# Cross attention's division: sums and weighted values copied off their banks by ScalarE, reciprocals in pairs over two steps

## Chip, core and metric

The kernel runs on one core of a Trainium2 chip. The metric is the device time of one execution in microseconds (us); before the change it is 1362.8 us, the median of three runs (1362.6 to 1363.32).

The core has engines that run side by side, each with its own list of instructions that it takes strictly in order: TensorE (PE; its weight loads are shown as PEld), VectorE (DVE), ScalarE (ACT), GpSimd (POOL), and SyncE (SP), which here issues DMA transfers. An instruction waits until what it needs is there, and everything behind it in its list waits with it. PE writes its results into banks of PSUM; a bank can be used again when the engine that reads it has read it.

## The reference, cut to what matters

A decoder layer in float32 on x of 16 batches x 112 tokens x 512: self attention, cross attention to a context of 375 tokens a batch, and a gated feed-forward network (FFN) with a Walsh-Hadamard transform. The change lies in the cross attention:

```python
q = proj(hs, Wq, bq, S)          # hs: layer norm of x; 16 heads of 32
k = proj(at, Wk, bk, T)          # at: the context, T = 375
v = proj(at, Wv, bv, T)
scores = einsum('bhsd,bhtd->bhst', q, k) / sqrt(32)
scores = clip(scores, -50.0, 50.0)
scores = where(attend, scores, -10000.0)
scores = clip(scores, -50.0, 50.0)
probs = softmax(scores, axis=-1)
probs = probs / (probs.sum(axis=-1, keepdims=True) + 1e-08)
ctx = einsum('bhst,bhtd->bhsd', probs, v)
delta = rs * (ctx @ Wo.T + bo)   # then a layer norm of delta, added to x
```

The kernel does not divide each probability. It multiplies the exponentials by the values, sums the exponentials over the 375 tokens, and multiplies the weighted values by the reciprocal of the sums and by 1/(1 + 1e-8).

## The kernel before

The program has three stretches: self attention (to about 300 us in the profile), cross attention (300 to 843 us), FFN (to the end). The order of PE's instructions is written by hand (a manual schedule, for PE alone): it is the order in which the program's lines are run. The order on the other engines comes from a scheduler, which goes by what is ready and by the order in the program; `tc.issue_after(x)` tells it not to place something ahead of instruction x.

In the cross attention the main loop goes over 16 batches b, and in a batch over three steps kc, each with 125 of the 375 context tokens (KC = 3, KP = 125). A head's 32 features lie in a group of 32 partitions, so that weighted values and sums are tiles of 128 partitions x 4 x 112 (C = 4, S = 112). One call of `Cross.step(b, kc)` does the following.

- PE makes the scores (L925) into two tiles of PSUM ("sc").
- ACT makes two exponentials from them (L1326, into es at kc = 0, into e otherwise) and two checks (L1330), which count scores beyond the limit in place; when both are done, the score banks are free.
- PE adds the weighted values of the step before ("late") to the bank "ys" (`weigh`, L936). There is one such bank.
- DVE adds the exponentials of the step before to those of its batch's first step (`add`, L1356, two instructions).
- When the step before was a batch's last, `divide` follows, so it stands in the step kc = 0 of the next batch: PE makes the sums over tokens (`key_sums`, L947) into one of three "mm" banks; DVE takes four reciprocals of it (L1368) into r, and multiplies the "ys" bank, the constant and r into xyT (L1369), the input of the output projection; ACT checks r (L1377).
- `f.fill(us)` then lets PE do some microseconds of other work, in pieces that all go through the three "mm" banks: the next batch's values (L898, copied from their bank to v by DVE at L903), its keys in seven products (L1005; DVE takes their results at L1058, L1069, L1082, L1086, L1089 and L1092), queries (L880, copied by ACT at L888), output projections of finished batches (L909), transposes of normalised rows (L841, L842), and products for half a W2 matrix of the FFN (L1627, copied by DVE at L1628).

DVE does more in the meantime: the sums of context quarters that the seven products want (L975), the norms' statistics and steps (L772, L773, L780 to L798, L1283 to L1295), and, in every step after `cross.last` (the last L1356), pieces of work on W2. For batches below 9 these are butterflies on half a W2 (L1643, L1644); at the end of each half SP stores it (L1649, and for the first half L1651), and DVE's L975 for a later batch, which uses a tile of the same pool, waits for that store. SP also loads the next half (L1616) and the context of a later batch (cT, L1214). From batch 9 on they are pieces of W2 (`W2Piece`): SP loads four quarters into w2i (L1660), DVE makes six combinations (L1671, L1674, L1677, L1680, L1683, L1686), SP stores each (L1669). L1671 is the first of a piece and so the one that waits for the loads; the loads wait until the piece before has done with the tile.

After the last step of batch 15, `weigh`, `add` and `divide` are called once more, and the FFN begins.

Of the kernel before, what the change touches and what calls it, by code (L numbers as in the profile page):

```python
# [14 lines left out]
AF = mybir.ActivationFunctionType  # L15
ALU = mybir.AluOpType
# [3 lines left out]
B, S, D = 16, 112, 512  # L20
# [3 lines left out]
C = D // P  # L24
# [6 lines left out]
GB = 4  # L31
# [572 lines left out]
def finite_layer(  # L604
# [30 lines left out]
    nc = tc.nc  # L635
# [12 lines left out]
    def psum(tag, shape, bufs=None):  # L648
        bufs = bufs or banks_of.get(tag, 2)
        return ps[""].tile(shape, F32, tag=tag, bufs=bufs, name=tag)  # L650
# [7 lines left out]
    def pair(name, tag="e", bufs=3):  # L658
        return evp.tile([P, 2, HG, S], F32, tag=tag, name=name, bufs=bufs)
# [66 lines left out]
    xyT = keep.tile([P, C, NT], F32, name="xyT")  # L726
# [9 lines left out]
    low, top = zero[:, : 2 * B * KC], zero[:, 2 * B * KC :]  # L736
    limit = keep.tile([P, 2], F32, name="limit")
# [70 lines left out]
    class Norm:  # L808


        def __init__(self, l, tiles):
            self.l, self.tiles = l, tiles
# [104 lines left out]
    def scores(k_of, q_of, rows_):  # L917

        scs = [psum("sc", [P, 2, 512]) for _ in range(2)]
        views = [  # L920
            s[:rows_, :, : HG * S].rearrange("p i (j s) -> p i j s", j=HG) for s in scs
        ]
        for j in range(C):
            for i in range(HG):
                nc.tensor.matmul(  # L925
                    views[i // 2][:, i % 2, j, :], k_of(i, j), q_of(i, j), start=True, stop=True
                )
        return views
# [16 lines left out]
    def key_sums(sums, es, n):  # L945
        for i in range(HG):
            nc.tensor.matmul(  # L947
                sums[ts(i, DH), :, :], ones[:n, :DH], es[i // 2][:n, i % 2], start=True, stop=True
            )
# [194 lines left out]
    class SelfAttention:  # L1144
# [35 lines left out]
        def step(self, b, grp, f, us, whole):  # L1180
            b, v, es = self.next
            if b + 1 < B:
                self.begin(b + 1, grp)
            first = max(0.45 * us, min(us, 5.5))
            f.fill(first)
            eTs = []
            for e, share in zip(es, (0.45 * (us - first), 0.35 * (us - first))):
                tr = psum("sc", [P, 2, 512])
                trv = tr[:S, :, : HG * S].rearrange("p i (j s) -> p i j s", j=HG)
                for i in range(2):  # L1190
                    for j in range(C):
                        nc.tensor.transpose(trv[:, i, j, :], e[:, i, j, :], ident[:S, :S])  # L1192
                eT = pair("eT")
                nc.scalar.copy(eT[:S], trv)
                eTs.append(eT)
                f.fill(share)
            y = psum("ys", [P, C, S])
            weighted_values(y, v[b % GB][:S], eTs, True, True)
            nc.scalar.copy(xyT[:, :, ts(b, S)], y)
            if whole:  # L1200
                f.drain()
            else:
                f.fill(0.2 * (us - first))
# [103 lines left out]
    class Cross:  # L1307
# [1 line left out]


        def __init__(self):
            self.late = None

        def step(self, b, kc, q, keys, f, us):
            scs = scores(
                lambda i, j: keys.k[ds(i * DH, DH), j, ts(kc, KP)],
                lambda i, j: q[ds(i * DH, DH), j, ts(b % 2, S)],
                KP,
            )
            n = b * KC + kc  # L1320
            late = self.late

            es = [(pair("es", "es", 3) if kc == 0 else pair("e"))[:KP] for _ in scs]
            self.late = (b, kc, keys.v[kc][:KP], es)
            for i, sc in enumerate(scs):
                nc.scalar.activation(  # L1326
                    es[i], sc, AF.Exp, scale=scl[:, n : n + 1], bias=bia[:, n : n + 1]
                )
            for i, sc in enumerate(scs):
                nc.scalar.activation(  # L1330
                    sc,
                    sc,
                    AF.Relu,
                    scale=nscl[:, n : n + 1],
                    bias=limit[:KP, :1],
                    accum_out=low[:KP, 2 * n + i : 2 * n + i + 1],
                )
            self.weigh(late)
            for i in range(2):
                self.add(late, i)  # L1340
            self.divide(late)
            f.fill(us)

        def weigh(self, late):
            if late is None:
                return
            b, kc, v, es = late
            if kc == 0:
                self.y = psum("ys", [P, C, S])
                self.es = es  # L1350
            weighted_values(self.y, v, es, kc == 0, kc == KC - 1)
# [8 lines left out]
        def divide(self, late):  # L1360
            if late is not None and late[1] == KC - 1:
                sums = psum("mm", [P, C, S])
                key_sums(sums, self.es, KP)

                b = late[0]
                r = ln.tile([P, C, S], F32, tag="r", name="r")
                for c in range(C):
                    nc.vector.reciprocal(r[:, c], sums[:, c])  # L1368
                nc.vector.scalar_tensor_tensor(  # L1369
                    xyT[:, :, ts(b, S)],  # L1370
                    in0=self.y,
                    scalar=1.0 / (1.0 + 1e-8),
                    in1=r,
                    op0=ALU.mult,
                    op1=ALU.mult,
                )
                nc.scalar.activation(  # L1377
                    r, r, AF.Relu, scale=-1.0, bias=limit[:, 1:], accum_out=top[:, b : b + 1]
                )

# [353 lines left out]
    for g in range(2, NG):  # L1736
        b = (g - 1) * GB
# [26 lines left out]
    cross = Cross()  # L1764
# [17 lines left out]
    for b in range(B):  # L1782
# [7 lines left out]
        if bl == 0:  # L1790
# [3 lines left out]
            elif g < 3:  # L1794
                c = AfterCross(whole[g - 1], n3[g - 1])
# [40 lines left out]
    cross.add(cross.late, 0)  # L1836
    cross.add(cross.late, 1)
    cross.divide(cross.late)
    ev.close()
    banks.close()  # L1840
    banks_of.update({"mm": 2, "ys": 2})
# [27 lines left out]
    def at_once(pieces):  # L1869
        run(pieces)  # L1870
        yield from ()

    def tiles_of(pieces):

        for _ in pieces:
            next(pieces, None)
            yield

    def tiles_of(pieces):
# [5 lines left out]
    late = itertools.chain(  # L1885
        itertools.repeat(None, 1),
        n3[2].transposes(),
        tiles_of(after[1].projections()),
        at_once(after[1].finish()),
        itertools.repeat(None, 3),  # L1890
        n3[3].transposes(),
    )
# [40 lines left out]
@with_exitstack  # L1933
def decoder_layer(ctx: ExitStack, tc: tile.TileContext, *args):
    nc = tc.nc
    flag = ctx.enter_context(tc.tile_pool(name="flag", bufs=1))
    unfit = flag.tile([1, 1], I32, name="unfit")
    finite_layer(tc, unfit, *args)
    with tc.If(nc.values_load(unfit, min_val=0, max_val=1, skip_runtime_bounds_check_because="a comparison gives 0 or 1") > 0):
        general_layer(tc, *args)  # L1940
# [49 lines left out]
```

## Time and profile before

| what | value |
|---|---|
| median of three runs | 1362.8 us |
| the profiled execution | 1362.72 us, its span 1360.9 us |
| granted PE clock, mean | 0.998 |
| cross attention, 300 to 843 us | 543.0 us, of them PE 539.1 busy, DVE 365.5, ACT 239.2 |
| reciprocals L1368 | 64, 795 ns median |
| product L1369 | 16, 624 ns median |
| check of r, L1377 | 16, 668 ns and 186 ns for its accumulator |
| exponentials L1326, checks L1330 | 1094 ns and 1068 ns mean |
| copy of values L903 | 0.68 us |

How to read it: the span is what the profiler shows between the first and the last instruction; the time of the execution is a little longer. A row of a timeline gives the start in us, the duration, engine and line, operation, the tile written and those read, the shape, how many in a row, and in brackets how long the engine was idle before it and what ended that. The name of a releaser is inferred from semaphores. PE's busy time is made of matmuls whose ends are modelled, so that a stall of under about a tenth of a microsecond can hide in it.

### The profile page before, as it was taken

The page shows a single profiled execution, that of the slowest core. Times are in us where ns is not written, and L with a number is a line of the kernel's source. Part 1 is how long each engine was busy: PE and PEld are TensorE (multiplying, and loading weights), DVE is VectorE, ACT ScalarE, POOL GpSimd, SP SyncE. Part 2 cuts the span into 40 slices and gives each one's busy share as a digit, 9 for nine tenths or more (in the row PEclk, how much of TensorE's full clock was granted, in tenths as well). Part 3 has the DMA queues.
Part 4 walks back from the last instruction along what each step waited for, and adds up shares of the span by engine and source line. Part 5 has one row for each costly group of instructions (what it writes and reads, how often), then busy time and mean ns, then how long its engine had stood idle before and what let it go on. Part 6 is the DMA issues. An engine that isn't in the chain of part 4 may idle for free.

```text
span 1360.9 us, 20404 instructions
## 1 busy us (share of the span) xinstructions
PE 1340.7 (99%) x8472; PEld 834.1 (61%) x8472; DVE 820.6 (60%) x1571; ACT 440.6 (32%) x859; POOL 38.0 (3%) x68
## 2 busy tenths in 40 slices
PE   8999999999999999999999999999999999999997
PEld 5587776665767577756777765545555555555553
DVE  4487768735565686669675668557653245554332
ACT  3355453643444334433545452201110011111000
POOL 2000100310000100000000000000000000000000
PEclk9999999999999999999999999999999999999999
DMA  7000022110103011103342111111031122322201
GB/s 249 1 1 1 22 80 71 31 47 24 55 24 124 16 55 62 55 1 109 108 136 97 39 48 32 47 46 47 32 124 62 47 62 70 92 77 79 92 0 57
DMA packets 63898, 82.44 MB, mean 61 GB/s; under 512 B 3105, under 2 KB 48177, under 8 KB 61365
## 3 DMA queue, kind: packets, MB, share of 16 engines
q1 hardware_dynamic: 62128, 77.83, 17.4%
q0 software_dynamic: 672, 1.62, 0.4%
q8 instruction: 69, 1.13, 0.3%
q10 hardware_dynamic: 996, 1.59, 0.3%
q14 instruction: 33, 0.26, 0.1%
HBM read 65.83 MB, written 15.20 MB: 60 GB/s over the span
## 4 chain that ended last, share of the span: by engine, by line
PE 94%; DVE 4%; ACT 1%; DMA 1%; issue 1%; DVEq 0%; ACTq 0%; POOLq 0%
PE mm L898 15%; PE mm L1005 14%; PE gate L1538 12%; PE mm L909 7%; PE ys L1538 7%; PE gate L1472 6%; PE mm L880 6%; PE mm L1538 5%; PE sc L925 5%; PE ys L936 4%; PE ys L1472 4%; PE mm L1472 3%; PE sc L1192 2%; PE mm L841 1%; PE mm L1627 1%; PE mm L947 1%
## 5 line engine op out<-in xcount | busy, mean ns | idle before, releaser
L898 PE MATMUL mm<-xv,cT 128*125 128x512 f32 x384 | 178.8, 602 | 0.8 <-DVE v L903 0.8
L1326 ACT ACTIVATE e<-sc,bia,scl 125x896 f32<-125x896 f32 x64 | 68.4, 1094 | 171.3 <-PE sc L925 171.3
L898 PEld LDWEIGHTS mm<-xv,cT 128*125 128x125 f32 x384 | 68.4, 187 | 76.4 <-issue 71.8
L1330 ACT ACTIVATE sc<-sc,limit,nscl 125x896 f32<-125x896 f32 x96 | 102.6, 1068 | 0.0
L1538 PE MATMUL gate<-t,f 128*128 128x448 f32 x256 | 101.5, 539 | 0.0
L1356 DVE TENSOR_TENSOR es<-es,e 125x896 f32<-125x896 f32 x64 | 68.4, 1090 | 49.1 <-ACT e L1326 49.1
L1472 PE MATMUL gate<-h,f 128*128 128x448 f32 x224 | 86.6, 540 | 0.0
L1538 PE MATMUL gate<-xyT,f 128*128 128x448 f32 x192 | 80.1, 540 | 0.0
L1538 PEld LDWEIGHTS gate<-t,f 128*128 128x128 f32 x256 | 48.8, 190 | 47.4 <-issue 46.9
L1162 ACT ACTIVATE e<-sc,mx 112x112 f32<-112x112 f32 x256 | 64.3, 402 | 41.7 <-DVE mx L1158 41.7
L1538 PE MATMUL ys<-t,f 128*128 128x448 f32 x192 | 77.4, 539 | 0.0
L1005 PEld LDWEIGHTS mm<-kt,xks 128*128 128x128 f32 x360 | 59.1, 190 | 15.3 <-issue 14.8
L1472 PEld LDWEIGHTS gate<-h,f 128*128 128x128 f32 x224 | 42.6, 190 | 41.2 <-issue 40.8
L1554 ACT COPY u<-gate 128x448 f32<-128x448 f32 x16 | 8.5, 531 | 182.3 <-PE gate L1538 109.4
L1005 PE MATMUL mm<-kt,xks 128*128 128x188 f32 x360 | 63.5, 324 | 0.0
L1538 PEld LDWEIGHTS ys<-t,f 128*128 128x128 f32 x192 | 36.6, 190 | 35.6 <-issue 35.4
L1484 DVE TENSOR_TENSOR h<-h,h 128x896 f32<-128x896 f32 x32 | 32.8, 1086 | 40.9 <-PE ys L1472 31.6
L1538 PEld LDWEIGHTS gate<-xyT,f 128*128 128x128 f32 x192 | 36.1, 190 | 34.3 <-issue 33.7
L898 PE MATMUL mm<-wv,xyT 128*112 128x512 f32 x128 | 56.9, 595 | 0.0
L925 PEld LDWEIGHTS sc<-q,kT 32*125 32x125 f32 x1536 | 46.2, 183 | 15.5 <-issue 13.2
L925 PE MATMUL sc<-q,kT 32*125 32x112 f32 x1536 | 54.7, 279 | 0.0
L1538 PE MATMUL mm<-xyT,f 128*128 128x448 f32 x128 | 53.4, 540 | 0.0
(237 smaller groups left out, 2211.2 us busy)
## 6 DMA issues: line engine op xcount, KB each, us to landing
f<-in_f_w SPq DMA_DIRECT2D x64, 256.0 KB, 3.2
f<-blocks SPq DMA_DIRECT2D x14, 1024.0 KB, 4.8
cT<-in_ctx SPq DMA_DIRECT2D x16, 750.0 KB, 4.8
w<-in_f_w SPq DMA_DIRECT2D x4, 1024.0 KB, 6.1
w<-w SPq DMA_DIRECT2D x4, 1024.0 KB, 4.6
w2i<-w SPq DMA_DIRECT2D x16, 256.0 KB, 4.1
blocks<-w2o SPq DMA_DIRECT2D x12, 256.0 KB, 2.4
blocks<-w2i SPq DMA_DIRECT2D x12, 256.0 KB, 2.4
```

What stands on the lines that cost most here:

```text
L880: nc.tensor.matmul(acc[:, :n], w[:, c, ts(j, P)], src[:, c, :], start=(c == 0), stop=(c == C - 1))
L898: nc.tensor.matmul(acc[:n, :], src[:, c, :], w[:, c, :], start=(c == 0), stop=(c == C - 1))
L909: nc.tensor.matmul(acc, xyT[:, c, ts(t, P)], w[:, c, :], start=(c == 0), stop=(c == C - 1))
L925: nc.tensor.matmul(views[i // 2][:, i % 2, j, :], k_of(i, j), q_of(i, j), start=True, stop=True)
L936: nc.tensor.matmul(y[ts(i, DH), j, :], v[:, HG * j + i, :], es[i // 2][:n, i % 2, j, :], start=first and j == 0, stop=last, skip_group_che ...
L1005: nc.tensor.matmul(acc[:, m], lhs[:, k, ts(m, P)], rhs[:, k], start=first and m == 0 and k == 0, stop=k == 1, skip_group_check=True,)
L1162: nc.scalar.activation(e[:, i, j, :], sc[:, i, j, :], AF.Exp, scale=SCALE, bias=mx[:, i, j : j + 1],)
L1326: nc.scalar.activation(es[i], sc, AF.Exp, scale=scl[:, n : n + 1], bias=bia[:, n : n + 1])
L1330: nc.scalar.activation(sc, sc, AF.Relu, scale=nscl[:, n : n + 1], bias=limit[:KP, :1], accum_out=low[:KP, 2 * n + i : 2 * n + i + 1],)
L1356: self.last = nc.vector.tensor_tensor(total, total, late[3][i][:KP], ALU.add).ins
L1472: nc.tensor.matmul(banks[m][bank], o[:, c, ts(m, P)], t[:, c, :], start=first and c == 0, stop=c == UNITS - 1, skip_group_check=True,)
L1538: nc.tensor.matmul(bank, o[:, s, k, :], t[:, k, :], start=first and k == 0, stop=k == 1, skip_group_check=True,)
```

## The change

`divide` keeps PE's sums and changes what follows. ACT copies the sums from their bank to r and the weighted values from "ys" to xyT, scaled by the constant; both banks are free after that. A generator, `quotients`, then holds the division in four parts: for each of the four blocks of 112 columns a reciprocal of r in place and a product of xyT with it, both in SBUF; behind the last part stands ACT's check of r. Two parts are laid in the batch's step kc = 1 and the rest in kc = 2, behind the L1356 adds of that step (`issue_after(self.last)`). Where the next batch is a multiple of GB = 4, all parts are laid at once in kc = 0, since an output projection over that batch's tiles follows; at the end of the stage too. The score checks L1330 now stand behind `weigh`, `add` and `divide` in the program.

```diff
-            self.late = None
+            self.late, self.parts = None, iter(())
...
                 nc.scalar.activation(
                     es[i], sc, AF.Exp, scale=scl[:, n : n + 1], bias=bia[:, n : n + 1]
                 )
+            self.weigh(late)
+            for i in range(2):
+                self.add(late, i)
+            self.divide(late)
             for i, sc in enumerate(scs):
                 nc.scalar.activation(
...
-            self.weigh(late)
-            for i in range(2):
-                self.add(late, i)
-            self.divide(late)
+            if kc == 0 and b % GB == 0:
+                for _ in self.parts:
+                    pass
             f.fill(us)
+            if b > 0 and kc > 0:
+                with tc.issue_after(self.last):
+                    for _ in range(2 if kc == 1 else C):
+                        next(self.parts, None)
...
-                for c in range(C):
-                    nc.vector.reciprocal(r[:, c], sums[:, c])
-                nc.vector.scalar_tensor_tensor(
-                    xyT[:, :, ts(b, S)],
-                    in0=self.y,
-                    scalar=1.0 / (1.0 + 1e-8),
-                    in1=r,
-                    op0=ALU.mult,
-                    op1=ALU.mult,
-                )
-                nc.scalar.activation(
-                    r, r, AF.Relu, scale=-1.0, bias=limit[:, 1:], accum_out=top[:, b : b + 1]
-                )
+                nc.scalar.copy(r, sums)
+                y = xyT[:, :, ts(b, S)]
+                nc.scalar.mul(y, self.y, 1.0 / (1.0 + 1e-8))
+                self.parts = self.quotients(b, y, r)
+
+        def quotients(self, b, y, r):
+            for c in range(C):
+                nc.vector.reciprocal(r[:, c], r[:, c])
+                nc.vector.tensor_tensor(y[:, c], y[:, c], r[:, c], ALU.mult)
+                yield
+            nc.scalar.activation(
+                r, r, AF.Relu, scale=-1.0, bias=limit[:, 1:], accum_out=top[:, b : b + 1]
+            )
...
     cross.divide(cross.late)
+    for _ in cross.parts:
+        pass
     ev.close()
```

By instructions: ACT has 32 more (16 copies, 16 scaled copies), DVE 48 more (64 reciprocals as before, 64 products in place of 16). PE's 9239 instructions and POOL's are the same in the same order. SP has the same 225 in another order: the store of the W2 halves (L1649) stands behind the loads L1616 or L1214 that it stood ahead of before.

## The prediction

> **What bounds it now.** First the page: engines' busy shares and the chain that ended last.
>
> ```profile
> span 1360.9 us, 20404 instructions
> PE 1340.7 (99%) x8472; PEld 834.1 (61%) x8472; DVE 820.6 (60%) x1571; ACT 440.6 (32%) x859; POOL 38.0 (3%) x68
> PE 94%; DVE 4%; ACT 1%; DMA 1%; issue 1%; DVEq 0%; ACTq 0%; POOLq 0%
> ```
>
> TensorE (PE) sets the end. Its order is written by hand and the change leaves it as it is, so only PE's idle time can change. Next, the window of the cross attention, with PE, PEld, DVE, ACT and POOL busy time, the clock and DMA.
>
> ```profile
> 300.00:843.00 543.00, 539.13 (x4909) 369.97 (x4908) 365.52 (x672) 239.22 (x368) 7.64 (x18) 1.00 0.19 61
> ```
>
> The granted clock is 1.00 and 543.00 - 539.13 = 3.87 us are idle; 0.73 of it lies before 333 and has nothing to do with the divisions. So no more than 3.1 us can be won. VectorE (DVE) is two thirds busy, ScalarE (ACT) under half. Then the view of PE's waits: what PE waited for, total, times, longest.
>
> ```profile
> PE mm L1005 <- DVE r L1368: 1.2, 2, 0.8
> PE mm L1627 <- DVE w L1628: 0.8, 1, 0.8
> PE mm L898 <- DVE v L903: 0.8, 1, 0.8
> PE mm L1005 <- DVE rstd L791: 0.3, 1, 0.3
> ```
>
> Only the first is for r, in two batches of sixteen. The timeline shows the larger (batch 13), then batch 10, which doesn't wait.
>
> ```profile
> 745.26 0.94 PE L947 MATMUL mm<-es,ones 125*32 125x448 f32 x8
> 749.17 2.98 DVE L1368 RECIPROCAL r<-mm 128x112 f32<-128x112 f32 x4
> 752.30 1.51 PE L1005 MATMUL mm<-cT,xk 128*128 128x188 f32 x8 [0.76 <-DVE r L1368]
> ```
>
> ```profile
> 658.88 2.99 DVE L1368 RECIPROCAL r<-mm 128x112 f32<-128x112 f32 x4 [2.63 <-PE mm L947]
> 663.91 0.69 DVE L1671 TENSOR_TENSOR w2o<-w2i 128x512 f32<-128x512 f32 x1 [2.04 <-DMA w2i<-w]
> 664.52 0.62 DVE L1369 SCALAR_TENSOR_TENSOR xyT<-ys,r 128x448 f32<-128x448 f32 x1
> 667.30 1.98 PE L898 MATMUL mm<-xv,cT 128*125 128x512 f32 x4
> ```
>
> In batch 13 the sums end at 746.20, DVE starts their reciprocals at 749.17 after other work, and PE wants the bank at 751.54. In batch 10 DVE waits 2.04 us for a DMA of W2 pieces (L1671), but the reciprocals already stand before it.
>
> **The prices.** A reciprocal from PSUM takes 2.98/4 = 0.745 us in a row (795 ns alone). From SBUF at 112 elements no row has it. Below: the 112x8 reciprocal in SBUF (L1174, 194 ns); above: the 795 ns. The slope between them, 601/104 = 5.8 ns an element, says that elements and not the source set it, so I take 0.73, near the upper end. The product L1369 takes 0.62. Its four successors have 112 elements in SBUF; rows of tensor_tensor in SBUF are 419 ns at 256 and 686 at 512, 1.04 ns an element, so 0.27 at 112, bounded by 0.42 above and by L773's 0.17 (six elements in) below. Two in a row overlap by 0.09 (L975: 543 ns each, 1.00 the pair), so 0.18 each in a row.
>
> DVE per batch, before: 4 x 0.73 + 0.53 = 3.45; after: 4 x 0.73 + 4 x 0.18 = 3.64; +0.2, and +0.5 by full durations. ACT gets two copies of 448 elements: L1199, the same shape from PSUM, takes 532 ns; 2 x 0.53 x 16 = 17 us on an engine busy 239 of 543.
>
> [...]
>
> **The moves, batch by batch.** (a) *The sums' bank.* ACT's order in the step becomes exp, limit check, product copy, exp, sums copy. In batch 13 the first check ends at 746.65; then 0.53, 1.0 and 0.53: the bank is free near 748.7, before the 751.54 at which PE wants it. So -0.76 in batch 13. Batch 9 likewise: -0.46, less 0.05 for a copy of v that nearly ties: -0.41. Elsewhere freeing it earlier wins nothing: PE didn't wait. Together -1.17.
>
> (b) *Batch 5.* Here DVE is full of norm work.
>
> ```profile
> 494.01 0.67 DVE L903 COPY v<-mm 125x512 f32<-125x512 f32 x1
> 494.74 1.98 PE L898 MATMUL mm<-xv,cT 128*125 128x512 f32 x4 [0.75 <-DVE v L903]
> ```
>
> The 0.28 at 489.48 goes. But after 486.35 the new order on DVE has, ahead of this copy of v: rstd steps 1.0, L1283 0.27, L1295 three times 2.0, statistics L772/L773 2.0, two reciprocals (1.45) with a product behind each (0.36), L1058 0.64, v twice 1.2: about 8.9, so the bank is free near 495.3, where PE, without the earlier stall, wants it at 493.7. Waits 1.65 in place of 1.03: +0.6 (0.3 to 0.9).
>
> (c) *Batch 10.* L1671 now stands ahead of the reciprocals. Behind it are queued two reciprocals, two products, v (L903), kT (L1058). The four loads of w2i wait for L1686, which ended at 656.25; ahead of it stand two more reciprocals with products from batch 9 (1.83, less 0.47 of slack: +1.36), so L1671 starts near 665.25. Then 0.6 + 1.45 + 0.38 + 0.68: the copy of v ends at 668.4, where PE wants it at 667.30: 1.1. The second v, behind two L1058 and two L1356 adds, ends near 671.7 against 670.4: a little more. +1.5 (0.5 if the loads land as early as before; 2.0 if the products take full durations).
>
> (d) *Batch 4.* The order of SP changes too: the store of the W2 half (L1649) falls behind the next W2 load (L1616) and the context load (L1214).
>
> ```profile
> 442.85 1.12 PE L1627 MATMUL mm<-w,bd 128*128 128x512 f32 x2 [0.80 <-DVE w L1628]
> 427.06 0.35 SPq L1649 DMA_DIRECT2D w<-w  x1
> 429.50 0.57 SPq L1214 DMA_DIRECT2D cT<-in_ctx  x1
> 440.13 1.01 DVE L975 TENSOR_TENSOR kt<-cT 128x376 f32<-128x376 f32 x2 [3.80 <-DMA blocks<-w]
> ```
>
> The last L1644 ends 2.8 us later, by batch 3's second pair of reciprocals, products and the work that they push; the store leaves about 430 and not 427. What DVE waits for at 440.13 lands 1.2 later, one L975 less (0.46) stands before L1628, so the wait of 0.80 grows to about 1.6: +0.9 with what follows (0.2 if DMA has room; 1.6 if the store pays its full delay). (e) *Batch 6.* The same store again: what DVE waits for at 509.64 lands behind both loads, up to 6 us later, near 515.7. The four sums L975 behind it (1.9) push the first L1628 to some 518.2, where PE wants its bank 2.7 after L1627's start at 515.03, at 517.7. +0.3 (0 if DMA has room, 0.7). (f) *Batch 15.* The checks end 1.06 later (two copies before them), so the score banks are late at 809.85: +0.2 (0 to 0.3). (g) Near ties of 0.2 us and less at L1086 and its kind in four batches: +0.4 (0.1 to 0.8). (h) The last batch divides at once; the gap before the FFN's work on DVE hides it: 0; without that cover, 0.2. The check on r moves behind the score checks; nothing waits for it.
>
> Sum: -1.17 + 0.6 + 1.5 + 0.9 + 0.3 + 0.2 + 0.4 = +2.7. The profiled execution took 1362.72 (span 1360.9, 1.8 around it), 0.08 under the median of 1362.8. Forecast 1362.72 + 2.7 = **1365.4 us**. Lower bounds give -1.17 + 1.1 = 0 (1362.7), upper ones -1.17 + 0.9 + 2.0 + 1.6 + 0.7 + 0.3 + 0.8 = +5.1 (1367.9).
>
> **Rivals.** *A, delay in every batch.* DVE may not start a reciprocal before ACT's sums copy, 2.5 us after the sums, and each product needs the reciprocal two places ahead; small dependent steps on DVE (L790 to L792, 0.16 us) start 0.2 apart, not 0.09. If each part takes 0.8 + 0.27 rather than 0.91, the pair before a copy of v is 0.3 to 0.4 late. It decides once that exceeds the slack of the v copy. For it: DVE waits 49 us for exps (L1356) in this kernel, so its order is strict. Against: most v copies have over 1 us of slack, and only one waited. 0.4 x 12 batches = 4.8, with the forecast's batch 10 included but (a) kept: 1367.5.
>
> *B, the gain without the bill.* The sums' bank is freed by ACT, DVE's lump of 3 us is in two, so the copies of v are on time: the waits of batches 9, 13 and 5 go (0.46 + 0.76 + 0.28 = 1.5), and the loads of w2i and W2 land as before. It decides if L1671 still starts by 663.9 and the store at batch 4 finds free DMA engines. 1361.2, down to 1359.6 if all 3.1 of idle time goes. Against it: the loads can't be issued before the work on DVE that frees their tile.
>
> *C, the change does little:* ACT's copies free the bank no earlier than DVE did (in batch 10: near 661.6 against 661.87), the losses stay under 1 us: 1362.7.
>
> **How the numbers follow.** The forecast's case has 0.60, A 0.20, B 0.13, C 0.07. What can be told from no change is 0.2%, 2.7 us, and the forecast lies on that line: of its 0.60 I put 0.38 beyond it and 0.22 within, since bounds reach further up than down from the line and the terms of (c) and (d) add up along one queue. All of A is slower. B gives 0.05 faster, 0.08 same; C 0.06 same, 0.01 slower by a queue not seen. Slower 0.59, same 0.36, faster 0.05. The likeliest case's own range is 1362.7 to 1367.9; B's better half and A's worse half may stay out: 1361.8 to 1368.4.
>
> **What would show it.** Right if, in the profile after, no PE wait names r or the copy; L1671 in batch 10 starts a microsecond later and PE waits over 1 us for v there; the wait at L1627 near 443 doubles; the wait for v in batch 5 is near 1.6. Wrong if PE's idle time in the stage falls below 3.9, or grows above 9 with waits in nearly all batches; or if ACT's copies come late enough that PE waits for them.

## The result and the profile after

The changed kernel takes 1373.68 us (median of four runs, 1371.54 to 1375.45), the kernel before 1362.7 beside it: the ratio is 1.008 with a 95% interval of 1.0063 to 1.0098. The forecast of 1365.4, with a range to 1368.4, had the side right and a quarter of the size: +2.7 forecast, +11 measured.

The profiled execution took 1372.77 us. Its page, span and engines' busy time first, then the chain that ended last:

```profile
span 1371.0 us, 20460 instructions
PE 1345.1 (98%) x8472; PEld 836.0 (61%) x8472; DVE 819.4 (60%) x1619; ACT 455.3 (33%) x891; POOL 38.4 (3%) x68
PE 89%; DVE 6%; DMA 3%; ACT 1%; issue 1%; SPq 0%; DVEq 0%; ACTq 0%; POOLq 0%
```

The span grew by 10.1 us. DMA's share of the chain went from 1% to 3%, and PE is busy for 4.4 us more with the same matmuls, which idle time cannot explain. PE's waits (what was waited for, total, times, longest):

```profile
PE mm L1634 <- DVE w L1635: 6.4, 3, 3.7
PE mm L898 <- DVE v L903: 2.9, 2, 1.8
```

L1634 and L1635 are the former L1627 and L1628, the W2 products. The waits for r are gone, as the change means them to be. The waits for W2 products, one of 0.8 before, are three with 6.4 in all. The largest, in the timeline after:

```profile
428.18 0.37 SPq L1623 DMA_DIRECT2D w<-in_f_w  x1
429.62 0.55 SPq L1214 DMA_DIRECT2D cT<-in_ctx  x1
430.21 0.61 SPq L1656 DMA_DIRECT2D w<-w  x1
430.86 0.43 SPq L1658 DMA_DIRECT2D blocks<-w  x1
442.71 1.01 DVE L975 TENSOR_TENSOR kt<-cT 128x376 f32<-128x376 f32 x2 [6.26 <-DMA blocks<-w]
443.21 5.92 POOL L849 TENSOR_TENSOR xr<-xr,beta 128x512 f32<-128x512 f32 x4 [4.87 <-DMA beta<-in_c_beta]
443.64 1.61 DVE L975 TENSOR_TENSOR kt<-cT,kt 128x376 f32<-128x376 f32 x1
445.17 1.27 DVE L1635 TENSOR_SCALAR w<-mm 128x512 f32<-128x512 f32 x2
445.90 1.13 PE L1634 MATMUL mm<-w,bd 128*128 128x512 f32 x2 [3.74 <-DVE w L1635]
446.96 1.51 PE L925 MATMUL sc<-q,kT 32*125 32x112 f32 x32
448.41 1.72 PE L936 MATMUL ys<-e,v 125*32 125x112 f32 x32
```

The first store of the W2 half (L1656) is issued at 430.21, behind two loads, where it left at 427.06 before. DVE's L975, which reuses the stored tile, waits until 442.71 and not 440.13. One L975 then takes 1.61 us in place of its usual 0.54, while GpSimd adds beta. PE, which wanted its bank at 442.16, gets it at 445.90.

Then look at what follows the wait: 32 scores take 1.51 us and 32 products of weighted values 1.72. In the profile before they took 1.14 and 0.97:

```profile
443.90 1.14 PE L925 MATMUL sc<-q,kT 32*125 32x112 f32 x32
444.97 0.97 PE L936 MATMUL ys<-e,v 125*32 125x112 f32 x32
```

The windows of the profile after show why (PE, PEld, DVE, ACT and POOL busy time, then the granted PE clock):

```profile
447.50:450.75 3.25, 3.25 (x64) 2.40 (x56) 3.25 (x6) 2.26 (x4) 1.64 (x2) 0.51 0.00 0
526.00:529.25 3.25, 3.25 (x50) 2.44 (x52) 3.21 (x6) 0.57 (x1) 0.00 (x0) 0.51 0.00 0
```

The second window lies behind the wait in batch 6:

```profile
520.33 2.74 PE L1634 MATMUL mm<-w,bd 128*128 128x512 f32 x6
522.61 1.01 DVE L975 TENSOR_TENSOR kt<-cT 128x376 f32<-128x376 f32 x2 [4.03 <-DMA w<-w]
525.32 1.36 PE L1634 MATMUL mm<-w,bd 128*128 128x512 f32 x2 [2.25 <-DVE w L1635]
```

After the waits of 3.74 us in batch 4 and of 2.25 us in batch 6, PE's clock is halved for some 3.4 us and then full again. At half speed 3.4 us do the work of 1.7: an estimate from the granted clock, beside which the 32 products above, all of them within the first stretch, took 1.72 us in place of 0.97.

The sum of the stage: PE's waits are 0.73 + 3.74 + 1.78 + 2.25 + 0.39 + 1.16 = 10.05 us, against 3.78 before: +6.27. Two slow stretches cost 2 x 1.7 = 3.4. Together 9.7 of the span's 10.1; the last 0.4 us were not traced. Over the whole program the mean granted clock of the four runs is 0.997, 0.996, 0.995 and 0.994, in the order of their times (1371.54, 1372.77, 1374.60 and 1375.45 us), so the length of the slow stretches goes with the spread of 4 us; only the profiled run, the second of these, has a trace that shows where they lie.

### The profile page after: what moved, and what is told of

Its sections match the earlier page's. It is cut to its first block, busy times and chain, and to the rows that moved or that the text cites. A ratio compares the mean times of both kernels' runs of the same rounds, so it can differ in the third digit from the quotient of the medians.

```text
span 1371.0 us, 20460 instructions
## 1 busy us (share of the span) xinstructions
PE 1345.1 (98%) x8472; PEld 836.0 (61%) x8472; DVE 819.4 (60%) x1619; ACT 455.3 (33%) x891; POOL 38.4 (3%) x68
## 3 DMA queue, kind: packets, MB, share of 16 engines
q8 instruction: 69, 1.13, 0.3%
q10 hardware_dynamic: 996, 1.59, 0.3%
## 4 chain that ended last, share of the span: by engine, by line
PE 89%; DVE 6%; DMA 3%; ACT 1%; issue 1%; SPq 0%; DVEq 0%; ACTq 0%; POOLq 0%
PE mm L898 15%; PE mm L1005 12%; PE gate L1545 12%; PE mm L909 7%; PE ys L1545 7%; PE gate L1479 6%; PE mm L1545 5%; PE sc L925 4%; PE mm L880 4%; PE ys L936 4%; PE ys L1479 4%; PE mm L1479 3%; PE sc L1192 2%; DMA w<-w 1%; PE mm L841 1%; DMA blocks<-w 1%
## 5 line engine op out<-in xcount | busy, mean ns | idle before, releaser
L1005 PEld LDWEIGHTS mm<-kt,xks 128*128 128x128 f32 x360 | 59.0, 190 | 15.3 <-issue 14.1
L1381 DVE RECIPROCAL r<-r 128x112 f32<-128x112 f32 x64 | 51.1, 827 | 23.8 <-ACT r L1374 23.8
L1005 PE MATMUL mm<-kt,xks 128*128 128x188 f32 x360 | 63.5, 324 | 0.0
```

What stands on the lines that cost most here:

```text
L1005: nc.tensor.matmul(acc[:, m], lhs[:, k, ts(m, P)], rhs[:, k], start=first and m == 0 and k == 0, stop=k == 1, skip_group_check=True,)
```

## The experiments

Two theories stood against each other: that the late stores did it (S), or the division itself, with ACT's copies ahead of DVE, small products and the spread (D). Times are medians, beside the kernel before on the same chip.

| run | time | before | ratio, 95% interval |
|---|---|---|---|
| e1, before with the stores held back | 1370.57 | 1362.34 | 1.0059 (1.0046 to 1.0072) |
| e2, after with the stores ahead | 1364.41 | 1362.34 | 1.0014 (1.0005 to 1.0023) |
| e3, all parts at once | 1368.49 | 1362.34 | 1.0055 (1.0036 to 1.0074) |
| e4, parts behind the W2 work | 1363.53 | 1362.34 | 1.0007 (0.9998 to 1.0016) |
| e5, after with filled waits | 1368.87 | 1362.53 | 1.0046 (1.0033 to 1.006) |
| e6, after without a beta addition | 1372.44 | 1362.53 | 1.0075 (1.0059 to 1.009) |
| e7, before with two copies | 1361.51 | 1362.53 | 0.9991 (0.9982 to 1.0) |
| e8, e7 with early stores | 1360.55 | 1362.53 | 0.9985 (0.9975 to 0.9994) |
| e9, e4 with early stores | 1362.74 | 1362.59 | 1.0 (0.9991 to 1.0009) |

**e1: the order of the stores alone, in the kernel before.** They are held behind the last load of a context, `kv[-1].load`.

```diff
-            nc.sync.dma_start(out=self.c[:, :, :S2], in_=ctx_t[b])
+            self.load = nc.sync.dma_start(out=self.c[:, :, :S2], in_=ctx_t[b]).ins
...
-            nc.sync.dma_start(out=halves[self.k], in_=self.w)
-            if self.k == 0:
-                nc.sync.dma_start(out=blocks2[4], in_=self.w)
+            with tc.issue_after(kv[-1].load):
+                nc.sync.dma_start(out=halves[self.k], in_=self.w)
+                if self.k == 0:
+                    nc.sync.dma_start(out=blocks2[4], in_=self.w)
```

> The kernel before with one edit: the stores of the W2 halves (L1649) are held behind the context load, so that SP issues them in the order of the kernel after. ACT and DVE do the work of before. Theory S (the stores): DVE's L975 near 442 and 515 waits 2 to 6 us longer, PE waits 3 to 4 us and about 2 us for the W2 products, and its granted clock falls to about 0.6 for some 3 us after each: 1368 to 1371 us. Rival D (the division itself: ACT's copies in front of DVE, products in four, pairs ahead of the values' copies): no change, 1362 to 1363.5.

Measured +8.2 us. The rows of PE that answer, in its timeline:

```profile
446.09 2.08 PE L1627 MATMUL mm<-w,bd 128*128 128x512 f32 x2 [4.06 <-DVE w L1628]
525.31 1.13 PE L1627 MATMUL mm<-w,bd 128*128 128x512 f32 x2 [1.59 <-DVE w L1628]
591.33 1.13 PE L1627 MATMUL mm<-w,bd 128*128 128x512 f32 x2 [0.29 <-DVE w L1628]
762.27 1.51 PE L1005 MATMUL mm<-cT,xk 128*128 128x188 f32 x8 [0.76 <-DVE r L1368]
```

These are after's three waits, in a kernel that divides as before and still has its wait for r. The clock is at 0.50 from 445.1 to 451.9 and from 527.0 to 530.4. (This is the slowest of the five runs, 1372.69 us.) The scheduler also moves some of DVE's instructions where they follow the stores. So the order of the stores is enough for most of the loss.

**e2: the order restored, in the kernel after.** The store is issued in the step of the last butterfly, and the next W2 load and context load stand behind it. One `yield` ahead of the store goes, and the context load is held in the same way as the W2 load.

```diff
...
-            nc.sync.dma_start(out=halves[self.k], in_=self.w)
+            stored.append(nc.sync.dma_start(out=halves[self.k], in_=self.w).ins)
+            yield
...
+            with tc.issue_after(stored[-1]) if b > 1 else nullcontext():
                 halves2.append(W2Half(b // 2 + 1))
...
```

> The kernel after with one edit: the stores are issued with the last butterfly, and the next W2 load and the context load are held behind them, so SP's order is that of before. The division stays as after. Theory S: the waits for W2 products shrink to under 1.5 us each and the clock stays at 1.00; 1363.5 to 1366 us, with the waits for v near 500 (1.8) and 681 (1.2) still there. Rival D: 1371 to 1375, as after.

1364.41: nine of the eleven microseconds gone, with the division untouched. In batch 6, where one store is made, it leaves ahead of both loads and the wait is gone. Batch 4 is not so clean a test. Its second store still stands behind both loads, as in the kernel before, and DVE's L975 starts even later than in the kernel after (442.71):

```profile
440.45 0.69 DVE L1635 TENSOR_SCALAR w<-mm 128x512 f32<-128x512 f32 x1 [4.03 <-PE mm L1634]
444.24 0.55 DVE L975 TENSOR_TENSOR kt<-cT 128x376 f32<-128x376 f32 x1 [3.10 <-DMA blocks<-w]
```

What spares PE there is DVE's order, which moved with the edit: a copy L1635 now stands ahead of the L975, and the bank is free. For batch 4 the evidence on the stores is that of e1, e4 and e9. PE's waits that are left:

```profile
445.45 0.96 PE L947 MATMUL mm<-es,ones 125*32 125x448 f32 x8 [0.49 <-DVE w L1635]
454.78 3.67 PE L909 MATMUL mm<-xo,xyT 128*128 128x512 f32 x8 [1.31 <-DVE xyT L1382]
496.50 1.98 PE L898 MATMUL mm<-xv,cT 128*125 128x512 f32 x4 [1.78 <-DVE v L903]
672.59 1.98 PE L898 MATMUL mm<-xv,cT 128*125 128x512 f32 x4 [0.74 <-DVE v L903]
```

The clock stays at 1.00. The waits for v belong to the division and stay, and one for its last products (1.31) is new.

**e3: copies and small products without the spread.**

```diff
-            if kc == 0 and b % GB == 0:
+            if kc == 0:
                 for _ in self.parts:
                     pass
             f.fill(us)
-            if b > 0 and kc > 0:
-                with tc.issue_after(self.last):
-                    for _ in range(2 if kc == 1 else C):
-                        next(self.parts, None)
```

> The kernel after, but all four parts laid at once in the step kc = 0 of every batch: ACT's copies and the four small products without the spread over two steps. SP's order is that of before by itself. Theory S: no wait for r or the sums' bank, W2 waits as before, 1361.5 to 1363.5 us. Rival D with ACT's copies as the cause: 1366 or more; with the spread as the cause: 1362 to 1363, which S and this form of D share, and which e2 tells apart.

A miss for S, which said 1363.5 at most: 1368.49, as the form of D said that blames ACT's copies. DVE and PE in batch 10:

```profile
664.76 0.69 DVE L1674 TENSOR_TENSOR w2o<-w2i 128x512 f32<-128x512 f32 x1 [7.74 <-DMA w2i<-w]
665.37 1.56 DVE L1377 RECIPROCAL r<-r 128x112 f32<-128x112 f32 x2
667.16 1.56 DVE L1377 RECIPROCAL r<-r 128x112 f32<-128x112 f32 x2
672.91 0.68 DVE L903 COPY v<-mm 125x512 f32<-125x512 f32 x1
673.64 3.66 PE L898 MATMUL mm<-xv,cT 128*125 128x512 f32 x4 [2.30 <-DVE v L903]
```

ACT's copy delays the reciprocals until they fall behind the instruction that waits for w2i (L1671 before, L1674 here). The kernel before has that instruction behind its reciprocals. The lump of four then makes v late by 2.30, and the clock halves again (0.50 from 673.6 to 677.1). In batch 15 ACT's check of r waits 2.69 us for the last product, the exponentials behind it are late, and PE waits 0.81 and 0.61 us for the score banks. The two fastest of the six runs, 1366.03 and 1366.80, have a mean clock of 0.999, as the kernel before has, and are still 3.7 and 4.5 us slower; that is about what PE's waits in the profile come to (7.5 us in the stage against 3.8 before). So D has a true part: the copy costs the reciprocals their place in DVE's queue, and in pairs this does less harm to v (1.16 in the kernel after, 0.74 to 0.90 in e2, e4, e6 and e9, nothing in e5) than in a lump.

**e4: the pairs behind the step's W2 work.**

```diff
                     for _ in range(1 if b < 9 else 2):
                         next(w2_work, None)
+                    for _ in range((0, 2, C)[kc] if b > 0 else 0):
+                        next(cross.parts, None)
```

(and they are no longer laid inside `step`).

> The kernel after, the pairs laid in the same steps but behind the piece of W2 work of that step and not ahead of it. SP's order is that of before again. Theory S: butterflies end as early as before, W2 waits under 1 us, 1361 to 1364 us. Rival D: the pairs still stand in kc = 1 and kc = 2 and ACT copies first, so 1368 or more.

1363.53 confirms S: the store leaves at 426.90. Its profiled execution is above the median (span 1365.2) and shows one wait that was expected to be under 1 us:

```profile
440.48 1.01 DVE L975 TENSOR_TENSOR kt<-cT 128x376 f32<-128x376 f32 x2 [3.87 <-DMA blocks<-w]
441.40 2.20 DVE L975 TENSOR_TENSOR kt<-cT,kt 128x376 f32<-128x376 f32 x2
444.26 1.47 PE L1630 MATMUL mm<-w,bd 128*128 128x512 f32 x2 [1.94 <-DVE w L1631]
```

The second pair of L975 began at 441.06 in the kernel before and took 1.13, most of it ahead of GpSimd's addition, which began at 441.78. Here the pair begins 0.34 us later, the addition at 441.94, and the second of them is slowed: 2.20. The wait becomes 1.94 in place of 0.80, and the clock is at 0.50 from 444.9 to 448.3. That profile is of the slowest of the eleven runs, 1366.95 us with a mean clock of 0.997; nine of the others, 1362.40 to 1363.61, have 0.998 or 0.999.

**e5: is it idle time that halves the clock?** 18 transposes of the identity stand ahead of the last W2 product of batches 3 and 5. These are the places of the waits of 3.74 and 2.25 us: they stand at the end of those batches, and the text elsewhere counts them to the batches that follow, 4 and 6.

```diff
+                if c == 6 and self.k in (1, 2):
+                    idle = psum("sc", [P, 2, 512])
+                    for k in range(18):
+                        nc.tensor.transpose(idle[:, 0, ts(k % HG, P)], ident, ident)
```

> The kernel after with 18 transposes of the identity (about 0.11 us each, 2.0 us in all, result unused) ahead of the last W2 product in batches 3 and 5, where PE waits 3.7 and 2.3 us. They add work and take no wait away. Theory C (PE's idle time brings the granted clock to 0.5 for about 3.4 us): the idle time left is under 1.8 us, the clock stays at 1.00, PE's busy time loses some 3.4 us of slow matmuls; 1369 to 1371.5 us, below after's 1371.5 to 1375.5. Rival: the low clock comes from something else (load, DMA): the time is that of after or up to 1 us more.

```profile
442.35 2.13 PE L1636 MATMUL sc<-ident 128*128 128x128 f32 x18
446.69 1.41 PE L1638 MATMUL mm<-w,bd 128*128 128x512 f32 x2 [2.21 <-DVE w L1639]
526.22 1.13 PE L1638 MATMUL mm<-w,bd 128*128 128x512 f32 x2 [0.46 <-DVE w L1639]
```

More work for PE, and less time: 1368.87, and its slowest run (1371.44) is still under after's fastest (1371.54). In batch 6, where 0.46 us of idle time is left, the clock stays at 1.00; in batch 4, where 2.21 is left (more than the 1.8 expected), it still falls, from 447.4 to 450.8. With the idle time of batch 6 filled its slow stretch is gone, so the idle time is the cause there; which idle time is enough is taken up below. The run saved 4.8 us in medians, where one slow stretch gives 1.7. But this profile, with a span only 1.3 under after's, is of the slowest run, with a mean clock of 0.997. The other four, 1368.38 to 1369.73, have 0.998 or 0.999, as the kernel before has, so little or nothing of a slow stretch is left in them. And one gain is not the filling's: the loads of w2i in batch 10 landed 1.4 us earlier beside PE's matmuls, and the wait of 1.16 for v is gone.

**e6: GpSimd's part.** The additions of beta for the last four tiles are left out.

> The kernel after without GpSimd's additions of beta for the last four tiles (L849; the output lacks beta there). Theory P (DVE's two-input operations slow down beside GpSimd's): DVE's L975 at 443.6 and 446.4, 1.6 us each, take 0.54, and PE's wait of 3.7 us for the W2 product falls to about 2.7: 1 to 1.5 us faster than after. Rival: the same durations without the additions, and no change.

```profile
443.73 0.54 DVE L975 TENSOR_TENSOR kt<-cT,kt 128x376 f32<-128x376 f32 x1
444.92 1.32 PE L1634 MATMUL mm<-w,bd 128*128 128x512 f32 x2 [2.91 <-DVE w L1635]
```

DVE's L975 is back from 1.61 to 0.54 and PE's wait from 3.74 to 2.91, so the slowing beside GpSimd is shown. The time of 1372.44 is 1.2 under after's, as expected, but it doesn't add to that: the runs of the two overlap, and the wait for v in batch 10 is shorter by 0.42 as well.

**e7 and e8: what there was to win.** Only batches 8 and 12, whose sums PE waited for in the steps of batches 9 and 13, get ACT's copy; e8 also issues both stores of the first half with its last butterfly, ahead of the two loads.

```diff
+                if b in (8, 12):
+                    nc.scalar.copy(r, sums)
+                    sums = r
                 for c in range(C):
                     nc.vector.reciprocal(r[:, c], sums[:, c])
```

> The kernel before with ACT's copy of the sums to r, and the reciprocals from there, in batches 8 and 12 alone, where PE waited 0.46 and 0.76 us for r; product as before. If these waits are all that the change can win: both vanish, nothing else moves, 1361.0 to 1361.8 us in place of 1362.3.

The second edit of e8 (one `yield` ahead of the stores goes as well), with the W2 load in batch 3 and the context load in batch 4 held behind `stored`:

```diff
...
-            nc.sync.dma_start(out=halves[self.k], in_=self.w)
+            stored = nc.sync.dma_start(out=halves[self.k], in_=self.w)
             if self.k == 0:
-                nc.sync.dma_start(out=blocks2[4], in_=self.w)
+                stored = nc.sync.dma_start(out=blocks2[4], in_=self.w)
+            self.stored = stored.ins
+            yield
...
+            with tc.issue_after(halves2[0].stored) if b == 4 else nullcontext():
                 kv.append(Keys(b + 2))
...
```

> As e7, and both stores of the first W2 half issued one behind the other with its last butterfly, ahead of the W2 load and the context load. Theory S: DVE's L975 near 440 starts some 3 us earlier and PE's 0.80 us of wait for the W2 product goes too: 1360.2 to 1361.2 us. Rival: the load of the next W2 half is late now and PE waits for it elsewhere: 1362 or more.

In e7 both waits for r are gone, and one of 0.17 us for v is new. In medians e7 is 1.0 us faster than before, with an interval that reaches 1.0; e8 is 2.0 us faster, the fastest of all and clear of the kernel before (0.9975 to 0.9994). In e8 DVE's L975 in batch 4 starts early:

```profile
434.76 1.01 DVE L975 TENSOR_TENSOR kt<-cT 128x376 f32<-128x376 f32 x2 [0.43 <-DMA blocks<-w]
```

PE's wait for W2 products is gone in that profile, and no wait for a load took its place.

**e9: the whole division with early stores.** The edits of e4 and the store edits of e8 stand together.

> The kernel of e4 (parts behind the W2 work) with the stores of e8. It has the whole new division and no late store. If the stores were the division's only large cost: PE's wait for the W2 product near 444 goes, the clock stays at 1.00, the waits for v near 497 (1.7) and 673 (0.9) stay: 1361.5 to 1363 us, above e8, which has not these two. Rival: the division costs more than its two waits for v: 1364 or more.

1362.74: the same as before. PE waits for v 1.66 and 0.90 us and twice 0.19 for kT; the wait at the W2 product is gone. In the profile before PE waited 1.22 us for r, 0.80 for the W2 product, 0.28 at a norm's step (L791) and 0.75 for v. So 2.30 us of waits are gone, of which the 0.80 is the work of the early stores and not of the division, and 2.19 are new, at v and kT. With its side effects removed the new division gives back there what it wins at r; e8, with early stores and two copies alone, is 2.2 us faster in medians.

## Why the prediction fell short

The signs that the prediction named as right were all seen: no wait for r or the copy, L1671 in batch 10 later by more than a microsecond, 1.78 us for v in batch 5, and a wait for the W2 product that at least doubled. What failed is what lay behind the last of them.

**(a) The sums' bank: right.** Both waits for r are gone, -1.22 where -1.17 was put. In batch 13:

```profile
758.83 0.54 ACT L1374 COPY r<-mm 128x448 f32<-128x448 f32 x1
760.99 1.56 DVE L1381 RECIPROCAL r<-r 128x112 f32<-128x112 f32 x2
762.15 1.44 PE L1005 MATMUL mm<-cT,xk 128*128 128x188 f32 x8
```

The copy ends at 759.37, 2.8 us before PE uses the bank.

**The prices: nearly right.** The rows of r, durations in ns (least, median, most):

```profile
L1381 DVE RECIPROCAL r<-r x64: 793/843/854, 347.6 to 836.1; 128x112 f32<-128x112 f32 x64
L1382 DVE TENSOR_TENSOR xyT<-xyT,r x64: 209/261/276, 349.1 to 837.0; 128x112 f32<-128x112 f32 x64
L1374 ACT COPY r<-mm x16: 522/543/545, 347.1 to 833.0; 128x448 f32<-128x448 f32 x16
```

The small product was put at 0.27 and takes 0.26, a pair 0.39; the copy 0.53 and 0.54. The reciprocal in SBUF was put at 0.73; alone it takes 0.84, and a pair 1.56. From PSUM the first two of the four in a row take 1.56 too, as the second starts 0.77 behind the first, and only those behind it follow at 0.71. So pair for pair there is no difference by source; cutting the row of four into pairs gave up the shorter steps. Four products in two pairs cost 2 x 0.39 = 0.78.

**(b) Batch 5: right.** The copy of v ended at 499.86, and PE waited 1.78 where 1.65 was put: +0.75 in place of +0.6. **(c) Batch 10: right in mechanism.**

```profile
674.79 0.69 DVE L1678 TENSOR_TENSOR w2o<-w2i 128x512 f32<-128x512 f32 x1 [7.50 <-DMA w2i<-w]
680.43 0.68 DVE L903 COPY v<-mm 125x512 f32<-125x512 f32 x1
681.16 1.98 PE L898 MATMUL mm<-xv,cT 128*125 128x512 f32 x4 [1.16 <-DVE v L903]
```

PE's matmuls there are 9.45 us later than before, so 674.79 answers to 665.34; 665.25 was put. Of the 1.5, 1.1 was put to the first copy of v, and PE didn't wait for that: its matmuls there (676.75) began before the copy did (677.18). The second copy, put at 671.7, ended at 681.11, which is 671.66 on before's scale, and PE waited 1.16 for it.

**(d) and (e) are the steps that failed.** The mechanism was named, the store behind the loads, but its price was not carried to the end. The text put +0.9 for batch 4 and +0.3 for batch 6; the waits grew by 2.94 and 2.25, with 0.39 more in batch 8, and each of the two large ones brought 1.7 us of slow matmuls: 9.0 us where 1.2 stood.

In batch 4 two things were mis-sized. What DVE waits for lands 2.6 us later, not 1.2: both stores, 1 MB each, now stand behind both loads, and the first had left ahead of them. The L975 that follows then fell on GpSimd's addition, which took another 1.1 us; in the profile before, the L975 were done ahead of that. The slowed one was DVE's L1643, with 1.66 us (0.68 in the median of its 24), and PE did not wait for it:

```profile
441.06 1.13 DVE L975 TENSOR_TENSOR kt<-cT,kt 128x376 f32<-128x376 f32 x2
441.78 5.69 POOL L849 TENSOR_TENSOR xr<-xr,beta 128x512 f32<-128x512 f32 x4 [3.55 <-DMA beta<-in_c_beta]
443.43 1.66 DVE L1643 TENSOR_TENSOR w<-w 128x512 f32<-128x512 f32 x1
```

The working shifted DVE's instructions without asking which other engine's they would now lie beside. Less 0.46 for the L975 that stands later: 0.80 + 2.6 - 0.46 + 1.1 = 4.0, measured 3.74.

In batch 6 the landing was put at 515.7 on before's scale. PE's L1634 began at 520.33 and not 515.03, so the two scales differ by 5.30, and DVE's L975 at 522.61 lies at 517.3: 1.6 later than put, and 7.7 later than the 509.64 of before. That the store would be behind both loads was seen; how late it lands was mis-sized. The 0.3 was the middle of bounds that ended at 0.7.

And nothing was put for the clock. In the profile before it is 1.00 in the whole stage, with waits of 0.8 at most; the sum took a wait to cost its own length, with bounds that shared this.

**(f), (g), (h):** no wait of more than 0.15 us, the least that the view lists, is seen for the scores of batch 15, at the near ties or at the end; 0.6 was put for them.

**The rivals.** A, delay in every batch, did not happen: DVE does wait 23.8 us for ACT's copy of r, as A said, but in 11 places with cover. B, the gain without the bill, needed the stores and loads in place, and even so (e9) the change wins nothing. C, little change, needed losses under 1 us, and the W2 waits alone are 6.4.

## What to carry to other kernels

When an edit delays work on one engine, follow the transfers that wait for it and ask not only when they start but what is issued ahead of them: here 2.7 us on DVE let two loads go first, and two stores landed 2.6 and 7.7 us later. Then ask what the delayed instruction will run beside, and how long TensorE stands still: the wait of 2.25 us in batch 6 cost some 4, by the estimate of 1.7 us for the halved clock behind it. And where a wait occurs in two batches of sixteen, change those two (e7, e8) and leave the other fourteen alone.

## What the runs showed of the hardware

- **TensorE's clock after an idle stretch.** The granted clock was at 0.50 for about 3.4 us after waits of 3.74 and 2.25 us (the kernel after), 2.91 and 2.35 (e6), 2.30 (e3), 2.21 (e5), 1.94 (e4) and 1.59 (e1), and for 6.8 us after one of 4.06 (e1). Waits of 1.16 and 1.78 (the kernel after), 1.31 and 1.78 (e2), 1.66 (e9), 1.67 (e4), 1.78 (e5) and 1.79 (e6) brought nothing: the matmuls behind them keep their durations, 1.44 us for eight L1005 and 1.14 for 32 scores. So length alone doesn't decide: 1.59 us was enough in e1 and 1.79 was not in e6. Where two falls occur in one execution, they begin 78.5 us apart in the kernel after (447.57 and 526.08) and in e6 (445.71 and 524.22), and 81.9 us apart in e1 (445.06 and 526.98): 23.0 and 24.0 times 3.41 us, the length of the first slow stretch in the kernel after (447.57 to 450.98). What decides beside the length was not shown.
- **DVE beside GpSimd.** L975, an operation of two inputs with 376 elements, takes 0.54 us; it takes 1.61 while GpSimd adds two tensors in SBUF (L849, 443.21 to 449.13 in the kernel after), and 0.54 again without that addition (e6). One-input L1635 takes 1.27 for two beside the same addition and 1.28 without it. The runs show the slowing and not its cause.
